# Two PSUM banks of a gated-graph kernel, cut by column halves instead of by gate part

## The chip, the cores and the metric

The kernel runs on one core of one Trainium2 chip. The metric is the device time of one launch in microseconds. Five engines matter: PE (matrix multiply), ACT (scalar engine), DVE (vector engine), POOL, and SP, which here only issues transfers. Matrix products are written into PSUM[...].

## The reference, cut to what matters

`x` is 128 graphs of 128 nodes with 256 features; `adj` holds one 128 x 128 matrix per graph. A first layer runs three steps of message passing with a GRU cell, a second layer is graph attention.

```python
h = relu(layernorm(x))
A = (adj != 0)
for i in range(3):
    m = einsum('bnd,de->bne', h, weight[i])
    a = einsum('bst,bsd->btd', A, m)
    r = sigmoid(a @ w_ir.T + h @ w_hr.T + b)
    z = sigmoid(a @ w_iz.T + h @ w_hz.T + b)
    n = tanh(a @ w_in.T + b_in + r * (h @ w_hn.T + b_hn))
    h = (1 - z) * n + z * h
x = x + h
h = relu(layernorm(x))
Wh = h @ W.T
e = leaky_relu((Wh @ a1)[:, :, None] + (Wh @ a2)[:, None, :])
x = x + softmax(where(adj == 0, -inf, e)) @ Wh
```

## The kernel before, in words

Four graphs make a group (`G = 4`), so 32 groups, each with a state `hT` of 256 features x 512 node columns (`T = 512`, `H = 256`), held as two chunks of 128 partitions. Each group goes through three GRU steps (`gru_step`, 96 in all) and then through `epilogue`, the attention layer. Two groups are worked on in turn, in two lanes: one step of one, one step of the other.

**The products of a step.** All of it is float32. A gate's 256 x 256 weight times the state is done as a 2 x 2 block product with seven smaller products in place of eight (sums of weights are made once, sums of the moving halves `t_h` and `t_a` in each step by `moving_sums`). One product of `product()` is three matmuls of 128 x 256, which the hardware runs as six. A step has two phases, each a call of `blocks`: phase 0 makes the reset gate r and the hidden part of n, phase 1 makes the update gate z and the given part of n. In both, index q = 0 is the gate (r or z) and q = 1 the part of n, side by side in a tile.

**The order on PE in a phase**, by the name of the weight block: W11 into `u`; S3 into `m7`; S2 added to `u`; W12; S1 added to `u`; N22 added to `c2`; S4. Between them stand copies on the other engines: after W11 ACT copies `u` into the low half of `c1` (L670); after S3 it copies `m7` to `m` in SBUF (L673); after S2 DVE writes `c2 = u + m` (L676); W12 is added to the low half of `c1`; after S1 ACT copies `u` into the high half of `c1` (L680) and DVE writes `c22 = u + m` to SBUF (L684); S4 is added to the high half of `c1`. Then W11 of the next phase may overwrite `u`.

So a phase leaves four quarter results: chunk 0 in `c1` (C11 in its low columns, C12 in its high columns), chunk 1 in `c2` (low) and `c22` (high). `c1` is one tile of two banks: the bank of q = 0 and the bank of q = 1, each with both column halves. `c2`, `u` and `m7` are one bank each, and three banks (`ps_misc`) serve everything else. [...]

**Who reads them.** In phase 0 ACT makes r by tanh (`reset`, L701) and v (`state_half`, L708) from `c22`, `c2` and `c1`; DVE then multiplies them (`candidate`, L598). In phase 1 DVE adds q = 1 to v (`add_half`, L741) and ACT makes z from q = 0 (`update`, L734). `state` (L606 to L614) turns v, z and the old state into the new one: a tanh on ACT, three operations on DVE for each chunk.

**What sets the order.** Each engine runs its instructions in program order, and the program order is made by a planner in the kernel, class `Order`. It keeps a time for each engine, adds a length for every piece (0.57 for an ACT copy of a bank, 0.62 for a DVE operation on a bank, 0.38 for half a bank, 1.3 for a product), and puts work that is ready (statistics, projections, transposes, epilogues of other groups) into the gaps (`fill`, `matmuls`, `finish`). `banks` holds the planned times at which `u`, `c1` and `c2` come free. Real waits are put in by the framework from what each instruction reads and writes.

**The transfers that matter here.** SP issues all of them, in one queue. A group's result row is stored (`out<-xt`) after its last attention product `po` (L944) and the addition to `xt` (L951); into the freed buffer the row of the group six further on is loaded (`xt<-in_x`), and its statistics (`st_a`, L406) follow on DVE. In the same queue stand sixteen small transfers for each transposition by blocks: `hT_a<-tq_a` at a group's start, `tq<-hT` and `prT<-e` in its epilogue. `prT` goes into the product `pq` (L566). The last two groups use transposes on PE in place of most of these.

Of the kernel before, what the change touches and what calls it, by code (L numbers as in the profile page):

```python
# [8 lines left out]
F32 = mybir.dt.float32  # L9
# [5 lines left out]
P = 128  # L15
# [3 lines left out]
T = G * P  # L19
H = T // 2  # L20
# [7 lines left out]
def preln_gnn_kernel(  # L28
# [14 lines left out]
    nc = tc.nc  # L43
# [5 lines left out]
    ps_sum = ctx.enter_context(tc.tile_pool(name="ps_sum", bufs=1, space=bass.MemoryType.PSUM))  # L49
# [7 lines left out]
    put = on_pe  # L57
# [78 lines left out]

    zero = borrowed(gate, [P, C, T], "r", "zero", T, bufs=1).bitcast(mybir.dt.bfloat16)[:, 0:T]
    put(nc.vector.memset(zero, 0.0))
    c1 = ps_sum.tile([P, 2, T], F32, name="c1")
    c2 = ps_sum.tile([P, 2, H], F32, name="c2")  # L140
    u = ps_sum.tile([P, 2, H], F32, name="u")
    m7 = ps_sum.tile([P, 2, H], F32, name="m7")
    for bank in (c1[:, 0, :], c1[:, 1, :], c2.rearrange("p g t -> p (g t)")):
        put(nc.tensor.matmul(bank, zero[:, 0:P], zero, start=True, stop=True))
    score_tiles = []
    for i in range(2):
# [16 lines left out]
    PE, ACT, DVE, DVE2, POOL, SP = "PE", "ACT", "DVE", "DVE2", "POOL", "SP"  # L163
# [118 lines left out]
    order = Order()  # L282
# [10 lines left out]
    S1, S2, S3, S4, N22, W11, W12 = range(7)  # L293
# [140 lines left out]
    def columns_tile(tag, name):  # L434
        return work.tile(
            [P, C, T], F32, tag=tag, name=f"{tag}_{name}", bufs=6 if tag == "hT" else 2
        )
# [156 lines left out]
    def candidate(s, r, v, ready):  # L594

        for o in (1, 0):
            s.v_ready[o] = yield DVE2, 0.62, ready[o]
            put(nc.vector.scalar_tensor_tensor(  # L598
                v[:, o, :], r[:, o, :], 1.0, v[:, o, :], ALU.add, ALU.mult
            ))  # L600
# [26 lines left out]
    def gru_step(s, last):  # L627

        name = f"{s.g}_{s.l}"
        l, hT, aT, tH, tA = s.l, s.hT, s.aT, s.tH, s.tA  # L630
        def half(X, c, n):
            return X[:, c, n * H : (n + 1) * H]

        hid, given = (s_hh, hT, tH), (s_f[l], aT, tA)

        def product(gates, to, weight, raw, sums, ready=0.0, first=False, close=()):

            for _, ends in gates:
                for _, _, t in ends:
                    if sums is not None:  # L640
                        order.finish([s.hidden, s.task], lambda: sums in t)
                        ready = max(ready, t[sums][1])
            for gate_no, ends in gates:
                for (_, there), _, _ in ends:
                    order.finish([*weights, *first_weights], lambda: (gate_no, weight) in there)
                    ready = max(ready, there[gate_no, weight])
            for q, (gate_no, ends) in enumerate(gates):
                for i, (S, X, t) in enumerate(ends):
                    moving = half(X, *raw) if raw else t[sums][0][:, sums, :]
                    put(nc.tensor.matmul(  # L650
                        to(q), S[0][:, gate_no, weight, :], moving,
                        start=first and q == 0 and i == 0, stop=(i == len(ends) - 1),
                        skip_group_check=True,
                    ))
            admit()
            done = order.take(PE, 1.3, ready)
            order.fill(done, close)
            order.matmuls(1.0)
            settle()
            return done  # L660

        def blocks(no, gates):

            m = gate.tile([P, 2, H], F32, tag="m", name=f"m_{name}_{no}")
            c22 = gate.tile([P, 2, H], F32, tag="c22", name=f"c22_{name}_{no}")
            done = product(gates, lambda q: u[:, q, :], W11, (0, 0), None, banks["u"], True, (ACT,))
            t = order.take(ACT, 0.57, max(done, banks["c1"]))
            put(nc.scalar.copy(c1[:, :, 0:H], u))  # L670
            done = product(gates, lambda q: m7[:, q, :], S3, None, T3, 0.0, True, (ACT,))
            tm = order.take(ACT, 0.57, done)
            put(nc.scalar.copy(m, m7))  # L673
            done = product(gates, lambda q: u[:, q, :], S2, None, T2, t, False, (DVE,))
            t = order.take(DVE, 0.62, max(done, tm, banks["c2"]))
            put(nc.vector.tensor_tensor(c2, u, m, ALU.add))  # L676
            product(gates, lambda q: c1[:, q, 0:H], W12, (1, 0), None)
            done = product(gates, lambda q: u[:, q, :], S1, None, T1, t, False, (ACT,))
            t = order.take(ACT, 0.57, done)
            put(nc.scalar.copy(c1[:, :, H:T], u))  # L680

            order.fill(t, (DVE,))
            tc22 = banks["u"] = order.take(DVE, 0.62, t)
            put(nc.vector.tensor_tensor(c22, u, m, ALU.add))  # L684
            done = product(gates, lambda q: c2[:, q, :], N22, None, T4, 0.0, False, (ACT, DVE))
            yield c22, tc22, done
            done = product(
                gates, lambda q: c1[:, q, H:T], S4, (1, 1), None, t, False, (ACT, DVE)
            )
            yield c22, tc22, done  # L690


        phase = blocks(0, [(0, (hid, given)), (2, (hid,))])
        c22, t22, done = next(phase)
        order.finish(first_weights)
        r = gate.tile([P, C, T], F32, tag="r", name=f"r_{name}", bufs=1)
        v = gate.tile([P, C, T], F32, tag="v", name=f"v_{name}")

        def reset(o, cols, src, length, ready):
            t = order.take(ACT, length, ready)  # L700
            put(nc.scalar.activation(  # L701
                r[:, o, cols], src, AF.Tanh, bias=brz[:, o : o + 1], scale=0.5
            ))
            return t

        def state_half(o, cols, src, length, ready):
            t = order.take(ACT, length, ready)
            put(nc.scalar.activation(  # L708
                v[:, o, cols], src, AF.Identity, bias=bhn[:, o : o + 1], scale=0.5
            ))  # L710
            return t

        low, high, full = slice(0, H), slice(H, T), slice(0, T)
        reset(1, high, c22[:, 0, :], 0.38, t22)
        reset(1, low, c2[:, 0, :], 0.38, done)
        banks["c2"] = state_half(1, low, c2[:, 1, :], 0.38, done)
        _, _, done = next(phase)
        reset(0, full, c1[:, 0, :], 0.6, done)
        banks["c1"] = state_half(0, full, c1[:, 1, :], 0.6, done)
        t1 = state_half(1, high, c22[:, 1, :], 0.38, t22)  # L720
        s.v_ready = [0.0, 0.0]
        half_task = order.add(0, candidate(s, r, v, (banks["c1"], t1)))


        phase = blocks(1, [(1, (hid, given)), (2, (given,))])
        c22, t22, done = next(phase)
        order.finish([half_task])
        order.finish(last)
        order.finish(weights[:2])
        z = gate.tile([P, C, T], F32, tag="z", name=f"z_{name}", bufs=1)  # L730

        def update(o, cols, src, length, ready):
            t = order.take(ACT, length, ready)
            put(nc.scalar.activation(  # L734
                z[:, o, cols], src, AF.Tanh, bias=brz[:, C + o : C + o + 1], scale=0.5
            ))
            return t

        def add_half(o, cols, src, length, ready):
            t = order.take(DVE, length, max(ready, s.v_ready[o]))  # L740
            put(nc.vector.tensor_tensor(v[:, o, cols], v[:, o, cols], src, ALU.add))  # L741
            return t

        add_half(1, high, c22[:, 1, :], 0.38, t22)
        update(1, high, c22[:, 0, :], 0.38, t22)
        tv = add_half(1, low, c2[:, 1, :], 0.38, done)
        banks["c2"] = update(1, low, c2[:, 0, :], 0.38, tv)
        s.halves = []
        new = columns_tile("hT", name)
        first = order.add(0.5, state(s, 1, hT, new, v, z, tv))  # L750
        _, _, done = next(phase)
        t = update(0, full, c1[:, 0, :], 0.6, done)
        t = banks["c1"] = add_half(0, full, c1[:, 1, :], 0.62, t)
        return [first, order.add(0.5, state(s, 0, hT, new, v, z, t))]

    banks = dict.fromkeys(("u", "c1", "c2"), 0.0)

    class Group:

# [222 lines left out]
    def settle():  # L982

        for i in range(2):
            lanes[i] = lanes[i] or enter(False)
# [22 lines left out]
    cols, rows_ = [P, C, T], [P, G, D]  # L1008
    wf_0 = [(gate, cols, "z", 1), (work, cols, "tq", 2)]
    reset, others = slice(0, 1), slice(1, 3)  # L1010
# [20 lines left out]
    while pending or waiting or lanes[0] or lanes[1]:  # L1031
# [3 lines left out]
        s = lanes[me] = lanes[me] or enter(True)  # L1035
# [48 lines left out]
```

## Time and profile before

| quantity | value |
|---|---|
| median of 3 runs | 2203.93 us (2202.45 to 2205.67) |
| profiled execution | 2205.54 us |
| span in its trace | 2203.8 us |
| DVE operation, 128x512 / 128x256 from PSUM (L741) | 688 / 419 ns |
| ACT read of 128x512 / 128x256 (L701) | 687 / 484 ns |
| same, L708 | 681 / 485 ns |
| same, L734 | 687 / 491 ns |
| ACT copy of a bank (L670, L680) | 580, 570 ns |
| one matmul of 128x256, drawn length | 379 ns, started 216 ns apart |
| granted TensorE clock | 0.997 |

A line of the groups or of the timeline names the engine, the source line of the kernel, the operation, the tile written and the tiles read, the shapes and how often. In a list of waits "A <- B: t, n, m" says that the instruction A waited for B for t us in all, n times, at most m us. Tiles whose names differ only in a number are shown under one name: `c` stands for `c1`, `c2` and `c22`. In the timeline the bracket at the end of a line gives the engine's idle time before the line's first instruction and what ended it. The span leaves out 1.7 us around the profiled execution.

### The profile page before, as it was taken

To read this page: it belongs to the slowest core of one execution; us is meant where nothing else is said; L and a number is where in the kernel's file an instruction comes from. 1 tells how busy PE (TensorE), PEld (TensorE's weight loads), DVE (VectorE), ACT (ScalarE), POOL (GpSimd) and SP (SyncE) were. 2 spreads that over 40 slices of the span, in tenths; PEclk is the share of its full clock that TensorE was granted. 3 is DMA by queue.
4 is the path that set the end of the run, shared out by engine and by line. 5 is a ranking of instruction groups with operands and counts; after the bars stand their busy time and mean duration, and the time that the engine had idled before them with its cause. 6 is when DMAs were issued, how large, how long until landed. Compare 5 with 4: busy or idle time off the path is not lost.

```text
span 2203.8 us, 32865 instructions
## 1 busy us (share of the span) xinstructions
PE 2176.6 (99%) x11259; PEld 1931.5 (88%) x11259; DVE 1744.5 (79%) x3960; ACT 1309.3 (59%) x2694; POOL 103.3 (5%) x204
## 2 busy tenths in 40 slices
PE   8999999999999999999999999999999999999997
PEld 7888888888888888888888888888888888888886
DVE  7678777788788878787888787887787888887866
ACT  5566656556566566656566565665655665656654
POOL 1000000000000000000000000000000000000000
PEclk9999999999999999999999999999999999999998
DMA  4001130131212212022210312213022021221101
GB/s 134 1 15 30 30 67 11 31 76 21 56 33 56 48 32 50 25 55 51 52 31 29 61 41 54 53 22 71 20 53 45 20 58 37 56 44 36 33 20 34
DMA packets 380936, 93.24 MB, mean 42 GB/s; under 512 B 325216, under 2 KB 376672, under 8 KB 380768
## 3 DMA queue, kind: packets, MB, share of 16 engines
q1 hardware_dynamic: 380768, 91.13, 19.1%
q8 instruction: 89, 1.46, 0.3%
q14 instruction: 79, 0.65, 0.1%
HBM read 35.92 MB, written 16.84 MB: 24 GB/s over the span
## 4 chain that ended last, share of the span: by engine, by line
PE 91%; DVE 4%; SPq 3%; DMA 1%; ACT 1%; issue 1%; DVEq 0%; ACTq 0%
PE u L650 31%; PE c L650 31%; PE m L650 10%; PE pa L566 7%; PE po L944 4%; SPq L60 3%; PE pq L566 3%; PE pr L483 2%; DMA xt<-in_x 1%; PE pw L348 1%; DVE v L741 1%; ACT z L734 0%; DVE c L684 0%; DVE hT L610 0%; DVE hT L608 0%
## 5 line engine op out<-in xcount | busy, mean ns | idle before, releaser
L650 PE MATMUL u<-t_h,s_hh 128*128 128x256 f32 x1152 | 343.5, 380 | 2.0 <-ACT c L670 2.0
L650 PE MATMUL u<-t_a,s_f 128*128 128x256 f32 x1152 | 311.3, 379 | 0.0
L650 PE MATMUL c<-aT,s_f 128*128 128x256 f32 x1152 | 311.3, 379 | 0.0
L680 ACT COPY c<-u 128x512 f32<-128x512 f32 x192 | 109.4, 570 | 325.8 <-PE u L650 294.3
L650 PEld LDWEIGHTS c<-aT,s_f 128*128 128x128 f32 x1152 | 218.9, 190 | 29.7
L650 PEld LDWEIGHTS u<-t_a,s_f 128*128 128x128 f32 x1152 | 218.9, 190 | 29.7
L650 PEld LDWEIGHTS u<-t_h,s_hh 128*128 128x128 f32 x1152 | 211.9, 190 | 33.8 <-ACT c L670 4.3
L741 DVE TENSOR_TENSOR v<-v,c 128x256 f32<-128x256 f32 (+1 forms) x288 | 139.5, 509 | 126.5 <-ACT z L734 121.5
L734 ACT ACTIVATE z<-c,brz 128x256 f32<-128x256 f32 (+1 forms) x288 | 159.8, 556 | 116.5 <-DVE c L684 67.4
L650 PE MATMUL c<-hT,s_hh 128*128 128x256 f32 x768 | 228.5, 379 | 0.0
L676 DVE TENSOR_TENSOR c<-u,m 128x512 f32<-128x512 f32 x192 | 134.3, 700 | 114.6 <-PE u L650 98.8
L701 ACT ACTIVATE r<-c,brz 128x256 f32<-128x256 f32 (+1 forms) x288 | 151.2, 552 | 91.8 <-DVE c L684 61.8
L684 DVE TENSOR_TENSOR c<-u,m 128x512 f32<-128x512 f32 x192 | 131.8, 687 | 69.2 <-ACT c L680 67.9
L673 ACT COPY m<-m 128x512 f32<-128x512 f32 x192 | 112.6, 587 | 100.4 <-PE m L650 100.4
L650 PE MATMUL m<-t_h,s_hh 128*128 128x256 f32 x576 | 171.5, 379 | 0.0
L650 PE MATMUL c<-t_h,s_hh 128*128 128x256 f32 x576 | 171.4, 379 | 0.0
L670 ACT COPY c<-u 128x512 f32<-128x512 f32 x192 | 111.3, 580 | 85.7 <-DVE v L741 71.9
L650 PEld LDWEIGHTS c<-hT,s_hh 128*128 128x128 f32 x768 | 144.7, 190 | 19.0
L590 ACT COPY aT<-pa 128x512 f32<-128x512 f32 x192 | 109.2, 584 | 84.6 <-PE pa L566 84.5
L650 PE MATMUL m<-t_a,s_f 128*128 128x256 f32 x576 | 156.1, 380 | 0.7 <-DVE t_a L445 0.7
L650 PE MATMUL u<-aT,s_f 128*128 128x256 f32 x576 | 155.6, 379 | 0.0
L650 PE MATMUL c<-t_a,s_f 128*128 128x256 f32 x576 | 155.6, 379 | 0.0
(122 smaller groups left out, 4188.0 us busy)
## 6 DMA issues: line engine op xcount, KB each, us to landing
xt<-in_x SPq DMA_DIRECT2D x31, 512.0 KB
out<-xt SPq DMA_DIRECT2D x31, 512.0 KB
tq<-hT SPq DMA_DIRECT2D x480, 32.0 KB
hT_a<-tq_a SPq DMA_DIRECT2D x448, 32.0 KB
at<-in_adj SPq DMA_DIRECT2D x32, 256.0 KB
e<-line SPq DMA_DIRECT2D x30, 256.0 KB
prT<-e SPq DMA_DIRECT2D x480, 16.0 KB
line<-turned SPq DMA_DIRECT2D x120, 0.5 KB
```

The lines of the kernel that those rows point to most:

```text
L566: put(nc.tensor.matmul(pa[:, k * P : (k + 1) * P], h[:, k, c * P : (c + 1) * P], A[:, k, :], start=True, stop=True,))
L590: put(nc.scalar.copy(aT[:, c, :], pa))
L650: put(nc.tensor.matmul(to(q), S[0][:, gate_no, weight, :], moving, start=first and q == 0 and i == 0, stop=(i == len(ends) - 1), skip_grou ...
L670: put(nc.scalar.copy(c1[:, :, 0:H], u))
L673: put(nc.scalar.copy(m, m7))
L676: put(nc.vector.tensor_tensor(c2, u, m, ALU.add))
L680: put(nc.scalar.copy(c1[:, :, H:T], u))
L684: put(nc.vector.tensor_tensor(c22, u, m, ALU.add))
L701: put(nc.scalar.activation(r[:, o, cols], src, AF.Tanh, bias=brz[:, o : o + 1], scale=0.5))
L734: put(nc.scalar.activation(z[:, o, cols], src, AF.Tanh, bias=brz[:, C + o : C + o + 1], scale=0.5))
L741: put(nc.vector.tensor_tensor(v[:, o, cols], v[:, o, cols], src, ALU.add))
L944: put(nc.tensor.matmul(po[:, j, :], hs[:, c, k * P : (k + 1) * P], gwt[:, c, :], start=(c == 0), stop=(c == C - 1),))
```

## The change

`c1` becomes a list of two tiles of one bank each. Tile 0 holds both q of the low columns, tile 1 both q of the high columns. `blocks` now yields three times per phase instead of twice: after W12 (tile 0 complete), after N22 (`c2` and `c22` as before), and after S4 (tile 1 complete). So every read of chunk 0 is of 128 x 256 values, twice as many. Tile 0 is read between W12 and S1: in phase 0 by ACT for r and for v; in phase 1 by ACT for z and then DVE for v. Tile 1 is read after S4: in phase 0 by ACT twice, in phase 1 by DVE first and then ACT. In phase 1 the calls `order.finish([half_task])`, `order.finish(last)` and `order.finish(weights[:2])`, which make sure that pending work of the step before has been issued, now stand after W12 instead of after N22; in phase 0 the same goes for `order.finish(first_weights)`. The planned lengths of 0.6 and 0.62 for the reads of chunk 0 become 0.38 each, and `banks` has an entry for each tile. The second state task now gets the time of the DVE addition instead of the later of two reads.

```diff
-    c1 = ps_sum.tile([P, 2, T], F32, name="c1")
+    c1 = [ps_sum.tile([P, 2, H], F32, name=f"c1_{n}") for n in range(2)]
...
-            t = order.take(ACT, 0.57, max(done, banks["c1"]))
-            put(nc.scalar.copy(c1[:, :, 0:H], u))
+            t = order.take(ACT, 0.57, max(done, banks["c1_0"]))
+            put(nc.scalar.copy(c1[0], u))
...
-            product(gates, lambda q: c1[:, q, 0:H], W12, (1, 0), None)
+            done = product(gates, lambda q: c1[0][:, q, :], W12, (1, 0), None)
+            yield done
             done = product(gates, lambda q: u[:, q, :], S1, None, T1, t, False, (ACT,))
-            t = order.take(ACT, 0.57, done)
-            put(nc.scalar.copy(c1[:, :, H:T], u))
+            t = order.take(ACT, 0.57, max(done, banks["c1_1"]))
+            put(nc.scalar.copy(c1[1], u))
...
+        reset(0, low, c1[0][:, 0, :], done)
+        banks["c1_0"] = state_half(0, low, c1[0][:, 1, :], done)
+        c22, t22, done = next(phase)
+        reset(1, high, c22[:, 0, :], t22)
+        reset(1, low, c2[:, 0, :], done)
+        banks["c2"] = state_half(1, low, c2[:, 1, :], done)
+        done = next(phase)
+        reset(0, high, c1[1][:, 0, :], done)
+        banks["c1_1"] = state_half(0, high, c1[1][:, 1, :], done)
         t1 = state_half(1, high, c22[:, 1, :], t22)
...
-        reset(0, full, c1[:, 0, :], 0.6, done)
-        banks["c1"] = state_half(0, full, c1[:, 1, :], 0.6, done)
...
-        c22, t22, done = next(phase)
+        done = next(phase)
         order.finish([half_task])
         order.finish(last)
         order.finish(weights[:2])
...
+        t = update(0, low, c1[0][:, 0, :], done)
+        banks["c1_0"] = add_half(0, low, c1[0][:, 1, :], t)
+        c22, t22, done = next(phase)
+        add_half(1, high, c22[:, 1, :], t22)
+        update(1, high, c22[:, 0, :], t22)
...
-        _, _, done = next(phase)
-        t = update(0, full, c1[:, 0, :], 0.6, done)
-        t = banks["c1"] = add_half(0, full, c1[:, 1, :], 0.62, t)
+        done = next(phase)
+        t = add_half(0, high, c1[1][:, 1, :], done)
+        banks["c1_1"] = update(0, high, c1[1][:, 0, :], t)
         return [first, order.add(0.5, state(s, 0, hT, new, v, z, t))]
```

More of the change, by code (lines that the diff above doesn't have):

```diff
@@ L142, in preln_gnn_kernel @@
     m7 = ps_sum.tile([P, 2, H], F32, name="m7")
-    for bank in (c1[:, 0, :], c1[:, 1, :], c2.rearrange("p g t -> p (g t)")):
+    for bank in (*c1, c2):
+        bank = bank.rearrange("p g t -> p (g t)")
         put(nc.tensor.matmul(bank, zero[:, 0:P], zero, start=True, stop=True))
@@ L687, in blocks @@
             done = product(
-                gates, lambda q: c1[:, q, H:T], S4, (1, 1), None, t, False, (ACT, DVE)
+                gates, lambda q: c1[1][:, q, :], S4, (1, 1), None, t, False, (ACT, DVE)
             )
-            yield c22, tc22, done
+            yield done
         phase = blocks(0, [(0, (hid, given)), (2, (hid,))])
-        c22, t22, done = next(phase)
+        low, high = slice(0, H), slice(H, T)
+        done = next(phase)
         order.finish(first_weights)
@@ L697, in gru_step, with reset @@
         v = gate.tile([P, C, T], F32, tag="v", name=f"v_{name}")
-        def reset(o, cols, src, length, ready):
-            t = order.take(ACT, length, ready)
+        def reset(o, cols, src, ready):
+            t = order.take(ACT, 0.38, ready)
             put(nc.scalar.activation(
@@ L704, in reset, with state_half @@
             return t
-        def state_half(o, cols, src, length, ready):
-            t = order.take(ACT, length, ready)
+        def state_half(o, cols, src, ready):
+            t = order.take(ACT, 0.38, ready)
             put(nc.scalar.activation(
@@ L711, in state_half @@
             return t
[L713 to L716, printed above, removed]
-        _, _, done = next(phase)
-        reset(0, full, c1[:, 0, :], 0.6, done)
-        banks["c1"] = state_half(0, full, c1[:, 1, :], 0.6, done)
-        t1 = state_half(1, high, c22[:, 1, :], 0.38, t22)
+        reset(0, low, c1[0][:, 0, :], done)
[7 more added lines that the diff above has]
+        banks["c1_1"] = state_half(0, high, c1[1][:, 1, :], done)
+        t1 = state_half(1, high, c22[:, 1, :], t22)
         s.v_ready = [0.0, 0.0]
-        half_task = order.add(0, candidate(s, r, v, (banks["c1"], t1)))
+        half_task = order.add(0, candidate(s, r, v, (banks["c1_1"], t1)))
         phase = blocks(1, [(1, (hid, given)), (2, (given,))])
-        c22, t22, done = next(phase)
+        done = next(phase)
         order.finish([half_task])
@@ L730, in gru_step, with update @@
         z = gate.tile([P, C, T], F32, tag="z", name=f"z_{name}", bufs=1)
-        def update(o, cols, src, length, ready):
-            t = order.take(ACT, length, ready)
+        def update(o, cols, src, ready):
+            t = order.take(ACT, 0.38, ready)
             put(nc.scalar.activation(
@@ L737, in update, with add_half @@
             return t
-        def add_half(o, cols, src, length, ready):
-            t = order.take(DVE, length, max(ready, s.v_ready[o]))
+        def add_half(o, cols, src, ready):
+            t = order.take(DVE, 0.38, max(ready, s.v_ready[o]))
             put(nc.vector.tensor_tensor(v[:, o, cols], v[:, o, cols], src, ALU.add))
             return t
[L744 to L747, printed above, removed]
+        t = update(0, low, c1[0][:, 0, :], done)
[3 more added lines that the diff above has]
+        update(1, high, c22[:, 0, :], t22)
+        tv = add_half(1, low, c2[:, 1, :], done)
+        banks["c2"] = update(1, low, c2[:, 0, :], tv)
         s.halves = []
@@ L750, in gru_step @@
         first = order.add(0.5, state(s, 1, hT, new, v, z, tv))
-        _, _, done = next(phase)
-        t = update(0, full, c1[:, 0, :], 0.6, done)
-        t = banks["c1"] = add_half(0, full, c1[:, 1, :], 0.62, t)
+        done = next(phase)
+        t = add_half(0, high, c1[1][:, 1, :], done)
+        banks["c1_1"] = update(0, high, c1[1][:, 0, :], t)
         return [first, order.add(0.5, state(s, 0, hT, new, v, z, t))]
-    banks = dict.fromkeys(("u", "c1", "c2"), 0.0)
+    banks = dict.fromkeys(("u", "c1_0", "c1_1", "c2"), 0.0)
     class Group:
```

## The prediction

> **What bounds the kernel now.** I read the page first, then the list of waits, then the gaps of PE one by one in the timeline, then a table of stretches.
>
> ```profile
> PE 2176.6 (99%) x11259; PEld 1931.5 (88%) x11259; DVE 1744.5 (79%) x3960; ACT 1309.3 (59%) x2694; POOL 103.3 (5%) x204
> ```
>
> PE is the bound. The change adds and removes no matmul, so only time in which PE stands can be won or lost. The table of stretches says where that is (columns after the times: length, then busy time and count of PE, PEld, DVE, ACT, POOL, then granted clock, DMA share, GB/s):
>
> ```profile
> 80.00:2140.00 2060.00, 2053.80 (x10691) 1830.25 (x10690) 1647.01 (x3680) 1238.79 (x2533) 89.84 (x171) 1.00 0.19 41
> 2162.50:2204.00 41.50, 26.06 (x120) 21.64 (x120) 26.42 (x83) 16.52 (x47) 2.93 (x6) 0.83 0.12 41
> ```
>
> In the long middle PE stands for 2060.0 - 2053.8 = 6.2 us; after its last gate product (at 2162.5) come 41.5 us of drain. Who stops PE, and who stops the engines that feed it:
>
> ```profile
> PE u L650 <- DVE c L684: 3.4, 5, 1.3
> PE u L650 <- ACT c L670: 2.0, 5, 0.4
> PE m L650 <- DVE t_a L445: 0.7, 4, 0.2
> ...
> DVE v L741 <- ACT z L734: 121.5, 96, 1.7
> ACT c L670 <- DVE v L741: 71.9, 89, 1.1
> ACT c L680 <- PE u L650: 294.3, 172, 5.6
> ```
>
> The reader should see two things. Once in each of the 96 steps DVE waits for ACT before it adds the second bank of c1, and 89 times ACT waits for that add before it may overwrite c1. Almost all of this is hidden: it reaches PE five times. One of the five, from the timeline:
>
> ```profile
> 456.76 0.43 DVE L406 BATCH_NORM_STATS2 st_a<-xt 128x6 f32<-128x256 f32 x1 [1.62 <-DMA xt<-in_x]
> 458.18 0.69 DVE L684 TENSOR_TENSOR c<-u,m 128x512 f32<-128x512 f32 x1
> 458.92 0.70 PE L650 MATMUL u<-hT,s_hh 128*128 128x256 f32 x2 [0.33 <-DVE c L684]
> 460.77 0.69 DVE L741 TENSOR_TENSOR v<-v,c 128x512 f32<-128x512 f32 x1 [1.12 <-ACT z L734]
> 461.55 0.57 ACT L670 COPY c<-u 128x512 f32<-128x512 f32 x1 [0.81 <-DVE v L741]
> 462.17 0.70 PE L650 MATMUL u<-t_h,s_hh 128*128 128x256 f32 x2 [0.40 <-ACT c L670]
> ```
>
> A load of x lands late, the statistics of it stand in DVE's queue ahead of c22 (L684), PE waits for c22, and the delay then runs on through z, v and the copy to c1 and stops PE a second time. True cost of such a gap: PE idle, plus 0.16 (matmuls start 0.22 apart but are drawn 0.38 long), plus 0.11 (two matmuls take 0.70 in place of 0.59). Five c22 gaps (0.33, 0.18, 0.47, 1.25, 1.14 idle): 3.4 + 5 x 0.27 = 4.7 us. Five copy gaps of 0.40: 3.35. Four t_a gaps of 0.17: 1.75.
>
> [...] ACT and DVE read different banks of the one tile and still take turns (the 121.5 us). [...] a statistic waiting for its load holds c22 behind it, as above. [...] The drain agrees: clock 0.83, and 16 pq matmuls take 3.62 us there against 1.78 in the stream.
>
> **The change part by part.** Per step, phase 0: one reset of 128x512 (0.687) becomes two of 128x256 (0.484), and so does state_half (0.681 against 0.485); phase 1: update likewise (0.687 against 0.491) and add_half (0.688 on DVE against 0.419). Added: ACT 96 x (0.281 + 0.289 + 0.295) = 83 us, DVE 96 x 0.150 = 14.4 us. ACT goes from 59 to 63%, DVE to 80%; both lie beside PE. What they could delay is the copy to c1 after S1 (L680, then L682), which S4 needs. Measured from the end of S1 the copy takes 0.26 to start and 0.57, then 0.1 to PE: 0.93 of the 1.29 that N22 covers, so 0.36 is free. The low half is read after W12: two reads, 0.26 + 2 x 0.44 = 1.14, done before S1 ends at 1.29; in phase 1 z then v, 0.26 + 0.49 + 0.42 = 1.17. ACT idles 325.8 / 192 = 1.7 us before L680 now. I cost this at nothing; without that cover, 0.1 us in each of 192 blocks would be 19 us.
>
> *At the end of S4.* Before: z of 128x512 0.26 + 0.69, v 0.69, copy 0.57, 0.1: 2.3 us of the 2.59 that W11 and S3 cover, in a step in which nothing is late. After: the high add waits for PE only (0.26 + 0.42), z follows (0.49), and the copy into the other tile waits only for W11: 1.29 + 0.26 + 0.57 + 0.1 = 2.2, with no reader of S4 in it. If c22 is late by d, before, the copy is late too; after, with c22 starting at c: adds to c + 1.2, z of c2 to c + 2.0, high add and z of c1 to c + 2.5, copy to c + 3.1, and S2 is due at c + 3.3. So the five copy gaps go (-3.35). The t_a adds stood behind v at L741 waiting for z; v now comes 0.7 us sooner, so the four t_a gaps go (-1.75).
>
> *What moves.* The kernel orders its queues by its own cost table, so the new lengths reorder everything. In the instruction order of the built changed kernel the schedule becomes regular: from the sixth group on, one pattern of two groups repeats 12 times. I used PE's work as a clock (0.216 us a hardware matmul) and counted from the last po of a group (which lets its row be stored and the next be loaded) to the S1 whose c22 stands behind the new statistics. The dangerous distance, 9.55 us, occurs 7 times before (five of these are the five gaps) and 13 times after. Price of one: four of the five gaps have the load wait; worked back from them, statistics start 10.5, 10.6, 11.1 and 11.3 us after po, and PE loses what exceeds 10.3 with the new queue (two statistics and an aggregate, 1.07, ahead of c22). That would be 0.2 to 1.0, mean 0.55. But the store there stood behind small transfers in SP's queue, 39.5 us of them against 37.4 us of PE work; after it is 42.9 against 41.1, so the store leaves 0.3 sooner, and most of the gaps are short: 0 to 0.7 each, I take 0.3. 13 x 0.3 = 3.9 in place of 4.7. The other transfers that PE or DVE await (prT, tq, hT_a) have the same or more distance in the new order (prT 14.0 us at least against 13.3 without a gap before).
>
> *The drain.* Before, group 29's pq and po come after the last product, and pq waits:
>
> ```profile
> PE ps L850 <- DVE junk L840: 5.4, 1, 5.4
> ...
> PE pq L566 <- DMA prT<-e: 3.5, 1, 3.5
> ```
>
> After, both stand before it: 1.78 + 3.46 = 5.2 us of PE work move ahead of the last product, and up to 1 us of wait with them (32 prT transfers in one row). Behind it the DVE chain is hidden state, two adds, statistics, scores: before, hidden state done at +5.6, rows added only from +10.7 behind po, scores through at about +22. After: state +6.3, rows +9.6, scores about +17 to +21. So the drain shortens by 5 to 12, less 6.2: -6 to +1, I take -2. Bounds -8 and +3, as the order of this stretch is all new.
>
> *Sum.* -3.35 - 1.75 - 4.7 + 3.9 - 2.0 = -7.9 us against the profiled execution (2205.54). That one lies 1.6 above the median of 2203.93; so 2203.9 - 7.9 = 2196.0.
>
> **Rivals.** (A) As above: 2196. Own range: gaps 0 to 0.7 each and drain -8 to +3, not all at one end: 2190 to 2203.
> (B) Given back: the 13 gaps cost 0.7 each (9.1) and the drain is as long as before: -9.8 + 9.1 = -0.7, 2203. For it: 99% busy PE leaves little, and the mean of the old gaps; against: the shorter SP row.
> (C) Slower: the repeated pattern repeats the late load 13 times at the price of the two dearest gaps (1.25 and 1.14 idle, so 1.5): 19.5 - 9.8 = +9.7, 2213.6. It decides from 1.1 us a gap on, that is when the load lands 11.4 us after po. For it: 11.3 was seen once; against: that was after another gap, and SP's row is shorter now.
> (D) Slower: the 288 more ACT instructions delay L682 past its 0.36 us; 0.1 us in half the blocks is 9.6 - 7.9: 2206. Against: the 1.7 us of idle.
>
> **How the numbers follow.** Chances: A 0.63, B 0.22, C 0.11, D 0.04. Below 0.2% (4.4 us) a measurement of this kernel cannot tell from no change. A gives 0.55 of faster and 0.08 of same; B mostly same (0.17, the rest faster 0.05); C slower, D mostly same or slower: faster 0.60, same 0.27, slower 0.13. The range is A's, stretched to B and the start of D: 2188 to 2206; C lies outside.
>
> **What would show it.** The wait of DVE v for ACT z of c1 and of ACT copy for DVE v gone from the list; no PE gap on the copy to c1 nor on t_a; 10 to 13 PE gaps on c22 some 134 us apart, each idle 0 to 0.5; pq of group 29 ahead of the last product and fewer than 39 us after it. The forecast is wrong if those gaps are 1 us or more, if PE waits for L682, or if the drain is over 43 us.

## The result, and the profile after

| | before | changed |
|---|---|---|
| median of 5 runs | 2203.93 us (2202.45 to 2206.58) | 2195.47 us (2194.34 to 2196.72) |
| ratio, 95% interval | | 0.996 (0.9947 to 0.9974) |
| profiled execution, span | 2205.54, 2203.8 us | 2195.40, 2193.5 us |

The kernel became 8.5 us faster; 2196 was forecast. That the sum came out does not mean that its terms did. First the page of the changed kernel, then its tables of stretches (length; then busy time and count of PE, PEld, DVE, ACT, POOL; clock, DMA share, GB/s):

```profile
PE 2172.2 (99%) x11259; PEld 1933.2 (88%) x11259; DVE 1754.7 (80%) x4056; ACT 1382.9 (63%) x2982; POOL 100.3 (5%) x204
```

```profile
80.00:2140.00 2060.00, 2060.00 (x10744) 1842.90 (x10743) 1666.33 (x3788) 1318.75 (x2833) 87.78 (x171) 1.00 0.19 41
```

```profile
0.00:80.00 80.00, 72.61 (x336) 57.95 (x337) 54.68 (x166) 43.23 (x95) 8.81 (x24) 1.00 0.30 92
2158.50:2193.50 35.00, 21.06 (x89) 15.97 (x87) 21.91 (x67) 13.54 (x41) 2.30 (x6) 0.78 0.09 31
```

In the middle PE no longer stands at all, as its work is drawn: 2060.00 of 2060.00. ACT and DVE do more and cost nothing. In the first 80 us PE is idle for 7.4, against 5.7 before (80 less 74.28 busy). After the last gate product come 35.0 us, against 41.5. Two things are mixed in this. The `pq` and `po` of group 29, 5.2 us of PE work at a clock of 1.00 (2140 to 2158.5 us), now stand ahead of the last gate product, as forecast. That product ends at 2158.5 (in the kernel before at 2162.3, counted from the starts of the matmuls); without the 5.2 us it would be 2153.3, so the stream of products ran 9.0 us faster. The drain changed by 35.0 + 5.2 - 41.5 = -1.3. Together that is -10.3, the difference of the spans.

The list of waits of the changed kernel, PE's first, then the pair that took turns:

```profile
PE pr_o L484 <- DVE hT L615: 5.5, 1, 5.5
...
PE pr L484 <- DVE hT L615: 1.1, 1, 1.1
PE pw L349 <- ACT wf L361: 0.8, 1, 0.8
```

```profile
ACT z L739 <- DVE v L746: 98.9, 186, 1.6
...
DVE v L746 <- ACT z L739: 73.3, 83, 2.9
```

PE's waits for `c22`, the copy to `c1` and `t_a` are gone. The turn-taking of ACT and DVE is not: for the high half ACT now waits for DVE (the 98.9 us also hold the waits on `c2`, 39.1 before), for the low half DVE still waits for ACT. The forecast had the latter gone from the list, although in the change itself z still goes first for the low half.

No `c22` reaches PE late, although the new order puts the new row's statistics ahead of it in twelve repeats of one pattern. This is the one that comes closest to being late, from the timeline:

```profile
457.74 0.43 DVE L407 BATCH_NORM_STATS2 st_a<-xt 128x6 f32<-128x256 f32 x1 [0.91 <-DMA xt<-in_x]
458.27 0.18 DVE L409 BATCH_NORM_AGGREGATE mv_a<-st_a 128x2 f32<-128x6 f32 x1
458.37 0.39 DVE L407 BATCH_NORM_STATS2 st_a<-xt 128x6 f32<-128x256 f32 x1
458.68 0.67 DVE L686 TENSOR_TENSOR c<-u,m 128x512 f32<-128x512 f32 x1
...
459.53 0.59 PE L651 MATMUL u<-hT,s_hh 128*128 128x256 f32 x2
```

DVE still waits 0.91 for the load. It keeps the order of its program: `c22`, whose copy (L682) was done at 457.71, starts at 458.68, behind the statistics. But it ends at 459.35, and W11 starts on time at 459.53. Counted from the end of `po` (447.55) the statistics start at +10.2. They may start as late as +10.3: that is the start of W11 less 0.05, less 0.69 for `c22`, less 0.94 for the statistics ahead of it.

### The profile page after: what moved, and what is told of

Its sections match the earlier page's. It is cut to its first block, busy times and chain, and to the rows that moved or that the text cites. A ratio compares the mean times of both kernels' runs of the same rounds, so it can differ in the third digit from the quotient of the medians.

```text
span 2193.5 us, 33318 instructions
## 1 busy us (share of the span) xinstructions
PE 2172.2 (99%) x11259; PEld 1933.2 (88%) x11259; DVE 1754.7 (80%) x4056; ACT 1382.9 (63%) x2982; POOL 100.3 (5%) x204
## 4 chain that ended last, share of the span: by engine, by line
PE 99%; DVE 1%; DMA 0%; ACT 0%; issue 0%; SPq 0%; DVEq 0%; ACTq 0%
PE c L651 34%; PE u L651 34%; PE m L651 11%; PE pa L567 8%; PE po L952 5%; PE pq L567 3%; PE pr L484 3%; PE pw L349 1%; DMA wih<-in_w_ih_t 0%; PE pt_a L462 0%; DVE hT L611 0%; DVE hT L609 0%; PE pp L916 0%; DVE hT L615 0%; DVE xt L959 0%
## 5 line engine op out<-in xcount | busy, mean ns | idle before, releaser
L739 ACT ACTIVATE z<-c,brz 128x256 f32<-128x256 f32 x384 | 185.5, 483 | 287.0 <-DVE v L746 98.9
L746 DVE TENSOR_TENSOR v<-v,c 128x256 f32<-128x256 f32 x384 | 154.7, 420 | 143.1 <-ACT z L739 73.3
L704 ACT ACTIVATE r<-c,brz 128x256 f32<-128x256 f32 x384 | 178.2, 480 | 137.2 <-PE c L651 93.6
L651 PEld LDWEIGHTS u<-t_h,s_hh 128*128 128x128 f32 x1152 | 216.3, 190 | 28.7 <-DVE v L746 0.2
L682 ACT COPY c<-u 128x512 f32<-128x512 f32 x192 | 109.4, 570 | 126.2 <-PE u L651 123.8
L711 ACT ACTIVATE v<-c,bhn 128x256 f32<-128x256 f32 x384 | 172.2, 476 | 0.0
```

Of the source, the lines that this page charges most:

```text
L651: put(nc.tensor.matmul(to(q), S[0][:, gate_no, weight, :], moving, start=first and q == 0 and i == 0, stop=(i == len(ends) - 1), skip_grou ...
L682: put(nc.scalar.copy(c1[1], u))
L704: put(nc.scalar.activation(r[:, o, cols], src, AF.Tanh, bias=brz[:, o : o + 1], scale=0.5))
L711: put(nc.scalar.activation(v[:, o, cols], src, AF.Identity, bias=bhn[:, o : o + 1], scale=0.5))
L739: put(nc.scalar.activation(z[:, o, cols], src, AF.Tanh, bias=brz[:, C + o : C + o + 1], scale=0.5))
```

## Experiments

Twelve kernels, each measured five times or more against the kernel before. Where it says so, the engines' instructions stand in the order of the kernel named, so that only lengths and waits differ. Where PE's order is the same in two kernels, their traces can be matched: the start of each matmul in one is compared with that of the same matmul in the other, and a step in the difference is time that PE lost or won there.

**E1, v first in the kernel before** (order unchanged on every engine):

```diff
-        t = update(0, full, c1[:, 0, :], 0.6, done)
-        t = banks["c1"] = add_half(0, full, c1[:, 1, :], 0.62, t)
+        t = order.take(ACT, 0.6, done)
+        t = banks["c1"] = order.take(DVE, 0.62, max(t, s.v_ready[0]))
+        (put v's addition, then z's tanh)
```

> The kernel before, with v (DVE) before z (ACT) for c1 at the end of phase 1; the order on every engine is that of before. Theory 'late load' (the loss starts where a late load holds c22 up, and runs on through the turn-taking of z, v and the copy): the copy gap shrinks from 0.40 idle to about 0.2 since z of c1 is still behind z of c2 on ACT, the four t_a gaps go: -5 x 0.2 - 1.75 = -2.8, about 2201; the five c22 gaps stay. Rival 'tile' (cutting the tile by columns is what brings the time): no change, 2204.

Measured: 2201.27, ratio 0.9987 (0.9981 to 0.9994). PE's list has `PE u L650 <- DVE c L684` five times, 3.2 us, and neither the copy nor `t_a`. The copy gaps went altogether, not by half, so the forecast of 2201 was met by its number and not by its terms. (In the short diffs, text in brackets stands for code.)

**E2, the cut alone**: two tiles by columns in the kernel before, four half reads after S4, z first; PE's and SP's order unchanged.

```diff
-        t = update(0, full, c1[:, 0, :], 0.6, done)
-        t = banks["c1"] = add_half(0, full, c1[:, 1, :], 0.62, t)
+        update(0, low, c1[0][:, 0, :], 0.3, done)
+        t = update(0, high, c1[1][:, 0, :], 0.3, done)
+        add_half(0, low, c1[0][:, 1, :], 0.31, t)
+        t = banks["c1"] = add_half(0, high, c1[1][:, 1, :], 0.31, t - HOP)
```

> The kernel before with c1 as two tiles by columns, but all four half reads where the two full reads stood, after S4, same planned lengths (4 x 0.3), so PE's and SP's order is that of before. Theory 'late load': the tile alone brings nothing, and behind S4 stand four ACT reads in phase 0 in place of two, about 0.4 us more before the copy to c1, which has some 0.1 us to spare there: a PE gap of about 0.3 in those phases where no other product fills in, half of 96: about +15, 2219 (2206 to 2235). Rival 'tile': the copy gaps go, 2195 to 2201.

Measured: 2201.85, ratio 0.9992 (0.9984 to 1.0001): a miss. The 15 us didn't come, and the copy gaps and `t_a` gaps went here too, which is the rival's mechanism; the interval just takes in no change. The timeline at the place shown in the prediction:

```profile
459.44 1.21 ACT L737 ACTIVATE z<-c,brz 128x256 f32<-128x256 f32 x3 [0.28 <-DVE v L744]
459.63 0.59 PE L651 MATMUL u<-hT,s_hh 128*128 128x256 f32 x2
460.06 0.59 PE L651 MATMUL m<-t_h,s_hh 128*128 128x256 f32 x2
460.31 0.79 DVE L744 TENSOR_TENSOR v<-v,c 128x256 f32<-128x256 f32 x2 [0.91 <-ACT z L737]
460.50 0.59 PE L651 MATMUL m<-t_a,s_f 128*128 128x256 f32 x2
460.82 0.57 ACT L671 COPY c<-u 128x512 f32<-128x512 f32 x1 [0.17 <-DVE v L744]
```

Three half reads take 1.21 us in a row, so they follow each other at about 0.37, not at the 0.48 that one is drawn. The copy starts when the low `v` is done and waits for no reader of the high half. Counted from W11 (here at 458.66, before at 458.92) it comes 0.47 sooner than before. Either of the two edits, E1 or E2, cuts the run-on; neither touches its start, the late `c22` (five gaps, 2.5 us here).

**E3, statistics behind c22** in the kernel before; among the engines' own orders only DVE's changed. From `held[0] = True` to `release()` the instructions of a new row's statistics are kept in a list:

```diff
+            held[0] = True
             done = product(gates, lambda q: u[:, q, :], S1, ...)
...
             put(nc.vector.tensor_tensor(c22, u, m, ALU.add))
+            release()
```

> The kernel before, with one thing moved: statistics of a newly loaded row that would be emitted between S1 and c22 are emitted behind c22 on DVE. Theory 'late load': the five c22 gaps (4.7) and the five copy gaps that follow from them (3.35) go, the four t_a gaps stay: -8.05, about 2195.9, as much as the whole change brought, with banks, reads and planner untouched. Rival 'tile' or 'turn-taking' (the 121.5 us of DVE waiting for ACT cost something by themselves): at most the c22 gaps go, 2199 or more.

Measured: 2211.21, ratio 1.0033 (1.002 to 1.0045): slower, a clear miss. Four of the five `c22` gaps are gone, but there are eleven gaps on the copy to `c1` (9.5 us) in place of five (2.0). One of the largest, from the timeline:

```profile
709.69 0.60 ACT L442 ACTIVATE h_a<-xt,nb_a,rstd_a 128x256 f32<-128x256 f32 x1 [2.60 <-POOL nb_a L433]
...
710.20 1.43 ACT L749 ACTIVATE z<-c,brz 128x256 f32<-128x256 f32 x3
...
711.65 0.69 DVE L756 TENSOR_TENSOR v<-v,c 128x512 f32<-128x512 f32 x1 [3.06 <-ACT z L749]
...
712.43 0.57 ACT L683 COPY c<-u 128x512 f32<-128x512 f32 x1 [0.81 <-DVE v L756]
...
713.05 0.70 PE L663 MATMUL u<-t_h,s_hh 128*128 128x256 f32 x2 [1.40 <-ACT c L683]
```

The delayed statistics delay POOL, POOL delays `h_a`, which stands ahead of z on ACT, and z delays `v` and the copy. What was moved out of one queue's way stood in another's. (The lines show this for one gap; the others were not followed back one by one.)

**E8, statistics behind the adds of v too** in the kernel before:

```diff
-            release()
+            if no == 0:
+                release()
...
         t = banks["c1"] = add_half(0, full, c1[:, 1, :], 0.62, t)
+        release()
```

The kernel also releases them earlier where ACT takes up a normalized row (`h`) while some are held.

> The kernel before, with the statistics of a loaded row that would be emitted between S1 of phase 1 and the end of the step put behind c22 and behind the adds of v on DVE (in the third run they stood behind c22 only, and held up the adds and so the copy to c1). Theory 'late load': neither c22 nor v waits for a load, so both the five c22 gaps (4.7) and the five copy gaps (3.35) go: 2196 (2194 to 2200), unless the state's operations, which now stand behind the statistics, are late. Rival (DVE has no place left for the statistics): 2204 or more.

Measured: 2208.08, ratio 1.0018 (1.0011 to 1.0025): by the time, the rival. But matched with the kernel before, PE regains 1.1 to 2.1 us at each of the five places of the late load, 7.4 in all, where 8.05 had been priced: the theory of these gaps and their price hold. It is at other places that `c2` (six gaps, 2.4 us) and again the copy (four gaps, 4.7 us) are late and more than that is lost. In the old order, pushing the statistics back in these two ways moved the loss and did not remove it.

**E4, one tile again and z first, in the changed kernel's order**:

```diff
-    c1 = [ps_sum.tile([P, 2, H], F32, name=f"c1_{n}") for n in range(2)]
+    c1_both = ps_sum.tile([P, 2, T], F32, name="c1")
+    c1 = [c1_both[:, :, 0:H], c1_both[:, :, H:T]]
...
-        t = add_half(0, high, c1[1][:, 1, :], done)
-        banks["c1_1"] = update(0, high, c1[1][:, 0, :], t)
+        (the same planned times; z emitted first, then v)
```

> The changed kernel with its order on every engine kept, but c1 one tile of two banks again (by q) and z before v for the high half: the turn-taking of ACT and DVE is back. Theory 'late load': c22 is never late in this order, so the waits are covered: 2195.5 within 1.5 of the changed kernel, though DVE waits tens of us for ACT. Rival 'tile': the time goes back, 2200 to 2204.

Measured: 2201.50, ratio 0.9989 (0.9981 to 0.9998): a miss, 6 us of the gain are gone with no `c22` late. Products matched with the changed kernel's show where: 2.6 us between 42 and 48 us (1.0 of a longer wait of PE for the state and 1.6 of a lower clock after it, 0.70 from 46 to 49 us, of which more at the end), 0.17 once in each of 13 periods of two groups, 0.5 at 336, and 1.3 in the drain. Two parts were undone at once, so E5 and E6 undo one each.

**E5, one tile, v first** (first part of E4's diff) and **E6, two tiles, z first** (second part):

> The changed kernel with its order on every engine and v before z kept, but c1 one tile of two banks by q again. Theory 'v first' (what the fourth run lost, 1.9 us before 48 us, some 17 times 0.17 and 1.4 in the drain, comes from v standing 0.35 us later behind z): v of the high half waits for nobody here either, so 2195.5 (2194 to 2197.5). Rival 'tile' (it is the two tiles by columns): 2199 to 2202, like the fourth run.

> The changed kernel with its two tiles and its order on every engine, but z before v for the high half of c1. Theory 'v first': v is late by 0.35 again at the start, once in a period of two groups and in the drain: 2201 (2199 to 2203). Rival 'tile': 2195.5 (2194 to 2197.5), as the copy to the low half waits for no reader of the high half.

Measured: E5 2195.03, ratio 0.9961 (0.9948 to 0.9973); E6 2201.11, ratio 0.9986 (0.9979 to 0.9992). The cut into two tiles is worth nothing in this order, with v first (E5 and changed, 0.4 apart) or with z first (E4 and E6, 0.4 apart). v first is worth 5.6 us with two tiles and 6.5 with one. In the profiled executions 1.6 of this is the lower clock near 46 us, in E6 as in E4.

**E7, the store in three transfers** in the changed kernel, to make its loads late:

```diff
-        dma(out[ks].rearrange("b t d -> t b d"), x1[:, part, :])
+        for a, b in ((0, 1), (1, 2), (2, n)) if n == G else ((0, n),):
+            dma(out[ks][a:b]..., x1[:, part.start + a : part.start + b, :])
```

> The changed kernel with every result row stored by three transfers in place of one, which puts two issues of some 0.55 us ahead of the next load in SP's queue. Theory 'late load': loads that land 9.2 to 10.2 us after po land 10.3 to 11.3 after it, c22 is then late at about 12 places by 0 to 1.0, mean 0.3 idle and 0.27 on top: +4 to +10, 2202 (2198 to 2206), and no gap on the copy to c1 nor on t_a follows. Rival 'runs on all the same': a copy gap of 0.67 after each of them, 8 more, 2207 or more. Rival 'loads don't matter': 2195.5.

Measured: 2198.73, ratio 0.998 (0.9971 to 0.999), 3.3 above the changed kernel, and no gap on the copy or on `t_a`. In the regular part five loads' statistics start more than 10.3 us after `po` (10.38 to 10.85), fewer than expected: where the three pieces go out at 1919.46, they take 1.51 us of SP in place of 0.56, and the statistics still start at +9.80. What makes the difference from load to load was not shown. At just these five places PE falls back in that part, by 0.2 to 0.6. The latest:

```profile
992.50 0.43 DVE L407 BATCH_NORM_STATS2 st_a<-xt 128x6 f32<-128x256 f32 x1 [1.56 <-DMA xt<-in_x]
...
993.44 0.67 DVE L686 TENSOR_TENSOR c<-u,m 128x512 f32<-128x512 f32 x1
994.17 0.70 PE L651 MATMUL u<-hT,s_hh 128*128 128x256 f32 x2 [0.37 <-DVE c L686]
```

`po` ended at 981.65; 992.50 is +10.85, 0.55 over the limit, and W11 comes 0.54 after the product ahead of it is done (its six matmuls start at 992.34 and take 1.29). So the limit is right, and at these five places a late `c22` does not run on. A sixth load, ahead of the regular part (statistics at 329.23), shows that it can: W11 comes 0.3 late there, and 5.5 us later S1 comes late by another 0.3, behind `c2`, which stands behind more statistics on DVE. The old run-on over z, v and the copy is gone; one over DVE's queue is still possible.

**E9, the old reads in the new order**, and **E10, the same with v first**: one tile, full reads after S4, planned times of the changed kernel, the order on PE, POOL and SP kept.

```diff
-        t = update(0, low, c1[0][:, 0, :], done)
-        banks["c1_0"] = add_half(0, low, c1[0][:, 1, :], t)
+        (planned times only)
...
-        (two half reads of the high columns)
+        (in E9 z, then v; in E10 v, then z)
+        put(nc.scalar.activation(z[:, 0, :], c1_both[:, 0, :], ...))
+        put(nc.vector.tensor_tensor(v[:, 0, :], v[:, 0, :], c1_both[:, 1, :], ALU.add))
```

> The instructions of the kernel before (one tile, full reads of 128x512, z before v) in the order on PE, POOL and SP that the planner made for the changed kernel: the order alone. Theory 'v first and short' (the new order is only as good as v is early): v ends about 1.0 us later after S4 than in the changed kernel, 0.5 later than in the fourth run, which lost 6: 2206 (2201 to 2214). Rival 'order' (the regular order brings the gain by itself): 2195 to 2199.

> The same, with v before z: one tile, full reads, v first, in the changed kernel's order; 288 instructions fewer on ACT and 96 fewer on DVE than the changed kernel. Theory 'v first and short': v ends 0.27 us later than in the changed kernel (0.69 in place of 0.42), as against 0.35 in the runs with z first, so most of their 6 us is lost again: 2200 (2197 to 2203). Rival 'v first alone': 2195.5 (2194 to 2197).

Measured: E9 2217.55, ratio 1.0058 (1.0046 to 1.0071), outside the theory's range on the slow side; E10 2197.68, ratio 0.997 (0.9958 to 0.9981). v first is worth 19.9 us here. In E9 PE waits for `c2` about twice in every period (28 times, 8.6 us idle). One of these waits, and the same place of the pattern in the changed kernel, four periods earlier, from the two timelines (E9 first):

```profile
1344.08 0.69 DVE L771 TENSOR_TENSOR v<-v,c 128x512 f32<-128x512 f32 x1 [1.29 <-ACT z L768]
...
1348.34 0.59 PE L651 MATMUL u<-t_h,s_hh 128*128 128x256 f32 x2
...
1349.87 0.69 DVE L677 TENSOR_TENSOR c<-u,m 128x512 f32<-128x512 f32 x1
...
1350.62 0.70 PE L651 MATMUL u<-t_h,s_hh 128*128 128x256 f32 x2 [0.39 <-DVE c L677]
```

```profile
794.32 0.42 DVE L746 TENSOR_TENSOR v<-v,c 128x256 f32<-128x256 f32 x1 [0.51 <-PE c L651]
...
799.36 0.59 PE L651 MATMUL u<-t_h,s_hh 128*128 128x256 f32 x2
...
800.06 0.70 DVE L677 TENSOR_TENSOR c<-u,m 128x512 f32<-128x512 f32 x1
...
801.08 0.59 PE L651 MATMUL u<-t_h,s_hh 128*128 128x256 f32 x2
```

The matmuls at 1348.34 and 799.36 are the last of S2; `c2` reads `u` after them, and S1 may add to `u` only when `c2` is done. Between `v` and `c2` DVE runs the same ten operations in both (`t_a`, `t_h`, three of the state), and in E9 without a break: `c2` starts 5.79 us after `v` starts there, 5.74 in the changed kernel. But v started late, after 1.29 us of waiting for z, so `c2` starts 1.53 after the last of S2 and not 0.70. This is the path by which v decides: whatever stands behind it on DVE moves with it. The order repeats it, so a delay that is too long for PE to cover is paid in every period: matched with the changed kernel, E9 loses 0.65 here each time, and 0.45 at a second place.

**E11, the low half read late** in the changed kernel: in both phases its reads stand right ahead of those of the high half.

> The changed kernel (two tiles, halves, v first) with the reads of the low half moved from behind W12 to right ahead of those of the high half, the rest of the order kept. Theory 'v first and short': DVE and ACT wait for S4 there anyway and the low half is ready, so it costs nothing: 2195.5 (2194 to 2198). Rival 'early read': 2199 or more.

Measured: 2206.03, ratio 1.0007 (0.9999 to 1.0016), 10.6 above the changed kernel: a miss. The list of waits points to the cause:

```profile
DVE v L769 <- ACT z L766: 74.3, 84, 0.9
```

L769 is `v` of the low half. There z still comes first, so the low `v` waits for it behind S4, and the high `v` stands behind the low one. PE falls back by 0.33 in each of 13 periods at the place shown for E9, S1 behind `c2`, so the same path is at work. That it is the place of z, and not that two adds stand there in place of one, is argued: the low half with v first was not run.

**E12, the last step's state by column halves** in the changed kernel, for a shorter drain (`state` with a `part`, four tasks instead of two, each pair's `epilogue` added when its half is done):

> The changed kernel with the new state of the last step of the last group made by column halves (eight short chains in place of four long operations for each half), so that the first pair of graphs can be turned to rows earlier: an attempt to shorten the drain. PE's wait of 5.5 us for the state falls to 3 to 4, the end comes 0 to 3 us sooner: 2194 (2192 to 2197).

Measured: 2196.82, ratio 0.9964 (0.9951 to 0.9976); span 2193.3 against 2193.5. Nothing was won, though the time lies in the range: PE still waits 5.5 us for the state, in two parts, and then 5.0 for the scores of another group (`ps` for `junk`), which fell behind. No version tried beats the changed kernel beyond the measurement; E5 equals it.

All of it in one table (us; medians of different sessions, in which the kernel before stood at 2203.86 to 2204.58):

| chunk 0 is read | z first | v first |
|---|---|---|
| order before, one tile, full reads | 2203.93 (before) | 2201.27 (E1) |
| order before, two tiles, halves late | 2201.85 (E2) | |
| new order, one tile, full reads | 2217.55 (E9) | 2197.68 (E10) |
| new order, one tile, low half early | 2201.50 (E4) | 2195.03 (E5) |
| new order, two tiles, low half early | 2201.11 (E6) | 2195.47 (changed) |

The new order with the old reads costs 13.6 (13.0 against the kernel before in its own session); v first takes off 19.9, the early half reads 2.6 more (E10 to E5), and the cut changes nothing (0.4). The shares depend on the path through the table: with z still first the early half reads take off 16.1 (E9 to E4), and v first then 6.5 (E4 to E5). Both make v end sooner, and most of the gain comes with the first of them. In the old order v first is worth 2.7. The empty cell was not run.

## Why the prediction was right, by its own steps

- *Copy gaps (-3.35) and t_a gaps (-1.75)*: gone, as forecast. The reason given for the copy, the other tile, is sufficient (E2) but not needed (E1, E5). Whether one tile with v first would also hold against a late `c22` in the new order was not tried.
- *"The t_a adds stood behind v ... v now comes 0.7 us sooner"*: the right mechanism, and its size was far off. It was priced by the four visible gaps. In the new order it is worth 5.6 (changed to E6), because `c2`, the start and the drain stand behind it on DVE: with z first PE waits 2.1 us for the state at the start (E6), not 1.1, and 6.5 in the drain (E9), not 5.5.
- *Statistics ahead of c22: 13 gaps at 0.3, 3.9 in all*: this term was mis-sized: it measured nothing. The 10 to 13 PE gaps of the forecast did not appear. The placements are there, and E7 confirms the limit of 10.3 us after the end of `po`. But the statistics that waited started at +9.5 to +10.2, where four of the old gaps had +10.3 to +11.1: the stores left 1.2 to 2.4 us after `po` in place of 2.0 to 2.8, a larger lead than the 0.3 in the forecast. Rival C's pattern did repeat; the latest of its twelve stayed 0.1 us short of costing anything. That is luck of this order, not a property of the change.
- *ACT's extra instructions at nothing*: right. PE waits for no copy (L682); the time that ACT waits for S1 ahead of this copy fell from 294 to 124 us and was enough. ACT's busy time grew by 74 us, not 83, since neighbouring reads overlap (at 400.89 two start 0.38 apart and are drawn 0.47 long). Rival D is out.
- *The drain -2.0*: -1.3 by the sum above.
- *Left out*: the start. PE is idle 1.7 us more in the first 80 us; E4 and E6 show that this stretch depends on v too.

On the profiled executions the terms were thus -3.35 - 1.75 - 4.7 + 0 in the middle, where the whole idle time went, +1.7 at the start and -1.3 in the drain: -9.4. Some 0.9 more, in shorter stalls that the forecast had not listed, makes the -10.3; it was not traced one by one. So the forecast of -7.9 counted 3.9 for loads that cost nothing, left out 1.7 at the start and took 0.7 too much for the drain; these errors cancel in part. What is left was hidden by the last step of the sum, which is at fault: the terms were priced on an execution of 2205.54 and taken off the median of 2203.93. Taken off the execution they were priced on, they say 2197.6, where 2195.40 came. That is still inside the range, but 2.2 off and not 0.5, so that the number came as close as it did is luck.

## What to carry to other kernels

When two engines read a product, let the one go first whose queue carries the chain to the next product: its partner's wait was free here, its own was worth 2.7 us in the old order and 6 to 20 in the new one. Price an operation that comes sooner or later by what hangs behind it on its engine, not by the gaps that show today, since a new order will have other ones. Where a planner orders the program by its own lengths, an edit is two changes, new instructions and a new order; run the old instructions in the new order before saying which of them brought the time.

## What the runs showed that was not expected

- PE's clock fell after a wait of some 2 us. In E6 PE stood idle for 2.14 us ahead of eight transposes (and 0.32 in the wait before), and then ran at 0.57 of full clock from 46 to 49 us, as a table of stretches shows:

```profile
43.00:46.00 3.00, 0.86 (x7) 0.69 (x7) 2.90 (x6) 0.57 (x1) 0.00 (x0) 1.00 0.00 0
46.00:49.00 3.00, 3.00 (x11) 2.35 (x10) 2.96 (x9) 1.24 (x3) 0.00 (x0) 0.57 0.00 0
```

  Pairs of matmuls start 0.86 apart there, not 0.43, which costs another 1.6 us. E4 (2.14 idle, then a clock of 0.70 in the same 3 us) and E9 (2.16, then 0.50) show the same; the changed kernel, with 1.12 us idle at that place, keeps its clock at 1.00. In E4 at least it was not the transposes that brought it, for there they run slowly from their start, 1.85 us for the eight against 1.06 in E6:

```profile
44.29 1.85 PE L484 MATMUL pr<-ident,hT 128*128 128x128 f32 x8 [2.14 <-DVE hT L615]
```

- Half reads on ACT follow each other at some 0.37 us although each is drawn with 0.48, so four of them cost less than the lengths say (E2).
- A delay of 0.17 us shows in no list: E4 loses it in each period with PE drawn as busy, because matmuls are drawn 379 ns long and start 216 apart, so that they overlap. It was found by matching the products of two traces.
